# Three of four gate tensors of a conditioned block: from a product with ones to a DMA broadcast and a copy

## The chip, the cores and the metric

The kernel runs on one core of a Trainium2 chip. The metric is the device time of one execution in microseconds (us). All numbers are float32.

A core has engines that run side by side and wait for each other with semaphores: TensorE (PE in the profile, with PEld for its weight loads), VectorE (DVE), ScalarE (ACT) and GpSimd (POOL). DMAs are issued here from the queues of SyncE (SP) and of ScalarE (ACTq). SBUF is the on-chip memory; PSUM is where TensorE writes its products.

## The reference

`x` is (2, 2048, 512), the condition `t` is (2, 512). One linear layer makes six rows of 512 for each batch element; two of the six are gates:

```
emb = silu(t) @ ada_w + ada_b
shift_msa, scale_msa, gate_msa, shift_mlp, scale_mlp, gate_mlp = split(emb, 6)
norm  = ln(x) * (1 + scale_msa) + shift_msa
x     = x + gate_msa * (gelu(norm @ ssm_w1 + ssm_b1) @ ssm_w2 + ssm_b2)
norm2 = ln(x) * (1 + scale_mlp) + shift_mlp
x     = x + gate_mlp * (gelu_tanh(norm2 @ ff_w1 + ff_b1) @ ff_w2 + ff_b2)
```

The hidden width is 512 in the first part (called A) and 1024 in the second (called C).

## The kernel before

**Blocks and stages.** The rows of x are cut into eight blocks of 512; blocks 0 to 3 belong to batch element 0, blocks 4 to 7 to element 1. A block i goes through `Norm` 1 (statistics on DVE, scales on POOL, normalisation on ACT, turning of 32x32 pieces on DVE, moves by DMA between partitions, modulation with scale and shift on ACT at L508), then `First` (hidden values hA_i), `residual` (oA_i), `Norm` 2, `Second` (hidden values hC_i) and again `residual` (oC_i). The result in the profile is named after the stage: py_hA, px_oC and so on, where y, x and v are PSUM banks.

**Products.** Every matrix product is done as seven products of half-size quarters, P1 to P7, with sums of quarters ahead of it (nS, hSA, hSC; made by POOL or DVE at L311) and additions behind it. For hC of blocks 1 to 7 a longer list of such sums is used (L650, L712). A stage takes a dictionary of hooks: lists of operations that are written into the program right after the product P1, P2 and so on. The schedule is manual, so the order in the source is the order of every engine's queue, and `hook(hooks, ("P6",), ...)` is how the work around a product is placed. The stages for blocks 0 and 1 are written out one by one; from block 1's hC on there is one loop over blocks.

**Gates.** A gate never multiplies the output: it is folded into the second weight matrix of its part (w2 for gate 2, the fw2 matrix for gate 5), row by row, by DVE at L359 (`weight_of_second`), and into the second bias (`gb`, L830, L869, L632). For that it must stand in all 128 partitions, as a 128x512 tile `pgate` in PSUM. There are four such tiles: gates 2 and 5 for batch element 0, used near 21 and 57 us, and for element 1, used near 246 and 338 us, when w2 and fw2 are loaded again and folded again. `rows_of_gates` multiplies silu(t), padded to 32 columns, with the gate's 512 columns of ada_w, one product for each quarter of the depth, in four groups of 32 partitions; DVE adds the bias rows, and `make_gate` puts one batch row on all partitions by a product with a matrix that holds ones at that row of each group:

```
r = work.tile([P, D], F32, tag="grows", name=f"grows_{g}", bufs=2)
nc.vector.tensor_tensor(r, pa, brows[:, (2, 5).index(g), :], ALU.add)
...
nc.tensor.matmul(pg, pick_bc[:, b, :], gate_rows[g], start=True, stop=True)
```

The rows of shift and scale come from `modulation` (L261), sixteen products of 32x128 for each, turned by DVE (L271).

**Queues at the start.** ACT's queue holds four small loads of condition and biases (L225 to L228), the two loads of gate-bias rows (L240), then the load of the activation table, a dummy activation (L764), silu (L782) and the first normalisations. SP's queue holds the large loads: x in two halves (L202), six pieces of ada_w (L208), the weights (L215), rows of bias put on all partitions (`load_row`, L219) and later the moves (L485) and the stores. PE runs five products that nobody reads (L774) while it waits for data.

## Time and profile before

| | |
|---|---|
| median of 3 runs | 603.66 us (603.02 to 604.52) |
| the profiled execution | 603.54 us |
| its span, first to last instruction | 601.7 us |
| PE busy | 592.5 us, 2827 matmuls |
| DVE, ACT, POOL busy | 376.1, 218.7, 397.1 us |
| DMA | 49.31 MB; mean busy share of the 16 DMA engines 0.8 to 0.9 up to 45 us, later 0 to 0.6 |
| gate products `pgate` (L299) | 4, in 8 records of 0.59 us (the second record of a product starts before the first is drained) |
| copies of gate tensors on ACT | none |

A line of the profile names a line of the kernel, the engine, the operation, the tile that is written and those that are read (without buffer numbers), and the shape. In views in order of time the first two columns are the start and the length in us, and the brackets at the end hold the time for which the engine was idle before and what it waited for. In the view of waits the columns are the total, the number and the longest, in us. "x8" behind a matmul are records: a float32 product leaves two.

### The profile page before, as it was taken

Reading aid. Unit: us, or ns where it says so; the run is one execution under the profiler, and the core shown is the slowest. Engines: PE = TensorE matmul, PEld = TensorE weight load, DVE = VectorE, ACT = ScalarE, POOL = GpSimd, SP = SyncE. Lnnn points to the kernel's source line nnn. Section 1 sums busy time; section 2 is a strip of 40 time slices with the busy share of each in tenths; the row PEclk is TensorE's granted clock in tenths of the full one; section 3 lists DMA queues with packets and bytes.
Section 4 is the critical chain, followed back from the end, with each engine's and each line's share of the span. In section 5 each row is a group of like instructions: output and inputs, shape, how many; then the busy total and the mean of one; then the engine's idle time right before and its main releaser. Section 6 shows DMA issues by size and latency. Waiting matters only on the chain.

```text
span 601.7 us, 8144 instructions
## 1 busy us (share of the span) xinstructions
PE 592.5 (98%) x2827; PEld 509.8 (85%) x2827; DVE 376.1 (63%) x638; ACT 218.7 (36%) x363; POOL 397.1 (66%) x459
## 2 busy tenths in 40 slices
PE   8999999999999999999999999999999999999997
PEld 4787887887888888888888888888888888888886
DVE  5978988997754475645754458644565336467642
ACT  3234247304532254323731346123553225212420
POOL 2878688998735896549978398885983695540110
PEclk9999999999999999999999999999999999999999
DMA  8980222300223003340051611321020300022001
GB/s 323 413 349 14 58 71 70 106 35 36 52 89 105 36 2 87 141 139 1 5 140 52 202 42 28 113 70 71 1 58 14 105 36 0 2 54 88 1 0 70
DMA packets 23116, 49.31 MB, mean 82 GB/s; under 512 B 4340, under 2 KB 4896, under 8 KB 22180
## 3 DMA queue, kind: packets, MB, share of 16 engines
q1 hardware_dynamic: 20032, 44.58, 22.3%
q10 hardware_dynamic: 3044, 4.23, 2.7%
q8 instruction: 22, 0.36, 0.2%
q14 instruction: 18, 0.15, 0.1%
HBM read 25.72 MB, written 8.39 MB: 57 GB/s over the span
## 4 chain that ended last, share of the span: by engine, by line
PE 92%; DVE 2%; DMA 2%; POOL 1%; issue 1%; ACT 1%; ACTq 1%; SPq 0%; DVEq 0%
PE py_oC L391 18%; PE px_hC L712 10%; PE pv_oC L391 9%; PE py_hA L391 9%; PE py_oA L391 8%; PE pv_hC L712 8%; PE py_hC L712 8%; PE px_oC L391 5%; PE pv_hA L391 4%; PE pv_oA L391 4%; PE px_hA L391 2%; PE px_oA L391 2%; DMA ada<-in_L_cond_ada_w_dram 2%; PE py_hC L391 1%; PE pv_hC L391 1%
## 5 line engine op out<-in xcount | busy, mean ns | idle before, releaser
L625 POOL TENSOR_TENSOR x<-x,gb 128x512 f32<-128x512 f32 x64 | 79.8, 1279 | 9.4 <-DVE gb L869 3.5
L508 ACT ACTIVATE nT<-nT,mod,mod 128x512 f32<-128x512 f32 x54 | 39.6, 802 | 103.1 <-DMA nT<-blocks 103.1
L311 POOL TENSOR_TENSOR hSC<-hClo 128x512 f32<-128x512 f32 (+1 forms) x34 | 39.6, 1169 | 45.9 <-ACT hClo L707 37.8
L465 ACT ACTIVATE nT<-x,nmr,rstd 128x512 f32<-128x512 f32 x56 | 42.5, 803 | 58.7 <-POOL nmr L452 42.8
L434 POOL TENSOR_SCALAR ve<-mv 128x4 f32<-128x4 f32 x16 | 3.7, 231 | 86.6 <-DVE mv L426 86.4
L391 PE MATMUL py_oC<-fw_s,hSC 128*128 128x256 f32 x256 | 57.9, 379 | 0.0
L391 PEld LDWEIGHTS py_oC<-fw_s,hSC 128*128 128x128 f32 x256 | 48.6, 190 | 6.6
L613 DVE TENSOR_TENSOR x<-py_oC,x 128x512 f32<-128x512 f32 (+1 forms) x36 | 22.5, 628 | 40.7 <-PE py_oC L391 40.7
L425 DVE BATCH_NORM_STATS2 st<-x 128x6 f32<-128x512 f32 x64 | 43.4, 678 | 5.1 <-DMA x<-in_x_dram 4.8
L712 PE MATMUL py_hC<-forms,fw 128*128 128x256 f32 x168 | 40.8, 379 | 0.0
L476 DVE STREAM_TRANSPOSE blocks<-nT 128x512 f32<-128x512 f32 x56 | 37.7, 693 | 3.9 <-ACT nT L465 3.4
L729 DVE TENSOR_TENSOR hClo<-hClo,py_hC 128x512 f32<-128x512 f32 x42 | 28.5, 681 | 17.1 <-ACT hClo L726 9.4
L650 POOL TENSOR_TENSOR forms<-forms 128x256 f32<-128x256 f32 x48 | 35.4, 738 | 2.8
L712 PEld LDWEIGHTS py_hC<-forms,fw 128*128 128x128 f32 x168 | 31.9, 190 | 4.3
L613 DVE TENSOR_TENSOR x<-py_oA,x 128x512 f32<-128x512 f32 x32 | 22.0, 689 | 19.6 <-PE py_oA L391 19.0
L729 DVE TENSOR_TENSOR hChi<-hChi,pv_hC 128x512 f32<-128x512 f32 x35 | 23.3, 683 | 17.1 <-PE pv_hC L712 17.1
L391 PE MATMUL py_oA<-w_s,hSA 128*128 128x256 f32 x128 | 30.4, 381 | 0.2 <-DVE x L613 0.2
L391 PE MATMUL py_hA<-nS,w_s 128*128 128x256 f32 x128 | 30.4, 381 | 0.0
L707 ACT ACTIVATE hClo<-hClo,colsT 128x256 f32<-128x256 f32 x56 | 25.3, 500 | 11.5 <-DVE hClo L729 11.4
L391 PE MATMUL py_oC<-fw,hClo 128*128 128x256 f32 x128 | 28.9, 379 | 0.0
L391 PE MATMUL pv_oC<-fw,hClo 128*128 128x256 f32 x128 | 28.9, 379 | 0.0
L391 PE MATMUL py_oC<-fw_s,hChi 128*128 128x256 f32 x128 | 28.9, 379 | 0.0
(210 smaller groups left out, 1406.2 us busy)
## 6 DMA issues: line engine op xcount, KB each, us to landing
nT<-blocks SPq DMA_DIRECT2D x168, 64.0 KB, 2.0
out_dram<-x SPq DMA_DIRECT2D x15, 512.0 KB, 3.0
x<-in_x_dram SPq DMA_DIRECT2D x7, 1024.0 KB, 7.1
ada<-in_L_cond_ada_w_dram SPq DMA_DIRECT2D x6, 1024.0 KB, 9.5
fw<-in_L_cond_ff_w_dram SPq DMA_DIRECT2D x3, 2048.0 KB, 9.1
nT<-blocks ACTq DMA_DIRECT2D x56, 64.0 KB, 2.0
w<-in_L_cond_ssm_w_dram SPq DMA_DIRECT2D x3, 1024.0 KB, 7.4
x<-in_x_dram SPq DMA_DIRECT2D x2, 512.0 KB, 5.1
```

The lines of the kernel that those rows point to most:

```text
L311: eng.tensor_tensor(out[:, r], a[:, r], b[:, r], f)
L391: nc.tensor.matmul(ps[b][j * apart][:, j, :], lhs(p, j, k), rhs(p, j, k), start=(fresh and j * (not apart) == 0 and k == 0), stop=(p in (" ...
L425: nc.vector.bn_stats(st, xs[self.i][:, c, :])
L465: nc.scalar.activation(t, x_c, AF.Identity, bias=self.nmr[:, c : c + 1], scale=self.rstd[:, c : c + 1])
L476: nc.vector.transpose(self.bl[:, :, :, c, :].rearrange("p m k q -> p k m q"), self.nT[:, c, :].rearrange("p (k m q) -> p k m q", k=KD, m=C),)
L508: nc.scalar.activation(dst, src, AF.Identity, bias=shift, scale=scale)
L613: nc.vector.tensor_tensor(d, ps[BANK[p]][:, js], d, ALU.add)
L625: lambda c=c: nc.gpsimd.tensor_tensor(xs[i][:, c, :], xs[i][:, c, :], gb, ALU.add)
L650: eng.tensor_tensor(reg[d], reg[a], reg[b], ALU.add if f == "+" else ALU.subtract)
L707: nc.scalar.activation(h, h, AF.Gelu_apprx_tanh, bias=fb1T[:, m : m + 1])
L712: nc.tensor.matmul(ps[b][:, j, :], fa[ra][:, j * P : (j + 1) * P], fb[rb].rearrange("p a (c q) -> p c a q", q=Q), start=(fresh and j == 0) ...
L729: nc.vector.tensor_tensor(dest(d), dest(d), ps[b], op)
```

## The change

Gate 2 of batch element 0 is still put on all partitions by a product. The other three go another way: SP stores the gate rows to a scratch in DRAM (`store_gate`, four small stores), loads one row of 2 KB back to all 128 partitions (`load_gate`, tile gsb), and ACT copies it to PSUM (`sent_gate`). The gate rows themselves are made by the same sixteen 32x128 products as shift and scale (`rows_of`), so that their bias rows have another layout: eight small loads on ACT's queue in place of two. The one remaining product becomes four of 128x128. The first gate 5 (`ff_gate`) moves from the hook P3 of hA_1 to a place behind hA_1 and the moves of block 0, and with it the folding of its bias (`gb5_0`, from P1 to P5 of oA_1) and POOL's additions of this bias to block 0 (P1 and P7, now all at P7); two of POOL's four additions of gate 2's bias to block 2 move from P1 of hC_0 into hC_1.

```diff
-    nc.gpsimd.memset(brows[:, :2, :], 0.0)
+    nc.gpsimd.memset(brows[:, 0, : 2 * P], 0.0)
+    gate_b = {}
     for n, g in enumerate((2, 5)):
-        nc.scalar.dma_start(
-            out=brows[:B, n, :], in_=ada_b[g * D : (g + 1) * D].unsqueeze(0).to_broadcast([B, D])
-        )
+        gate_b[g] = brows[:, 0, n * P : (n + 1) * P]
+        for m in range(P // G):
+            row = ada_b[g * D : (g + 1) * D].rearrange("(n m q) -> m n q", n=KD, q=G)[m]
+            nc.scalar.dma_start(
+                out=gate_b[g][m * G : m * G + B, :].rearrange("p (n q) -> p n q", n=KD),
+                in_=row.unsqueeze(0).to_broadcast([B, KD, G]),
+            )
...
     def rows_of_gates(g):
...
+        pa = rows_of(g)
+        r = work.tile([P, P], F32, tag="grows", name=f"grows_{g}", bufs=2)
+        nc.vector.tensor_tensor(r, pa[:, :P], gate_b[g], ALU.add)
         gate_rows[g] = r
-    def make_gate(g, b):
+    def make_gate(g):
+        pg = ps_t.tile([P, D], F32, tag="t", name=f"pgate_{g}_0")
+        to = pg.rearrange("p (n m q) -> p m n q", n=KD, q=G)
+        for m in range(P // G):
+            nc.tensor.matmul(to[:, m], pick[:, m, :], gate_rows[g], start=(m == 0), stop=(m == P // G - 1))
+        gate[g, 0] = pg
+    def store_gate(g):
+        t = dram.tile([B, D], F32, tag=f"gdr_{g}", name=f"gdr_{g}")
+        to = t.rearrange("b (n m q) -> m b n q", n=KD, q=G)
+        for m in range(P // G):
+            rows_m = gate_rows[g][m * G : m * G + B, :].rearrange("p (n q) -> p n q", n=KD)
+            nc.sync.dma_start(out=to[m], in_=rows_m)
+        gate_dram[g] = t
+    def load_gate(g, b):
+        t = work.tile([P, D], F32, tag="gsb", name=f"gsb_{g}_{b}", bufs=1)
+        gate_sb[g, b] = load_row(t, gate_dram[g][b])
+    def sent_gate(g, b):
         pg = ps_t.tile([P, D], F32, tag="t", name=f"pgate_{g}_{b}")
-        nc.tensor.matmul(pg, pick_bc[:, b, :], gate_rows[g], start=True, stop=True)
+        nc.scalar.copy(pg, gate_sb[g, b])
         gate[g, b] = pg
...
-    hook(hooks, ("P6",), fold2(1, 7))
+    hook(hooks, ("P6",), fold2(1, 7) + [lambda: store_gate(2)])
...
-    hook(hooks, ("P6",), [lambda: rows_of_gates(5)])
+    hook(hooks, ("P6",), [lambda: rows_of_gates(5), lambda: store_gate(5)])
...
-    hook(hooks, ("P3",), [ff_gate])
...
+    load_gate(5, 0)
     n2[0].move((nc.scalar,), (2, 3))
+    ff_gate()
...
-    hook(hooks, ("P1",), hA_sums[2:3] + [gb5_0] + fw1_sums[3:] + gb5[:3])
+    hook(hooks, ("P1",), hA_sums[2:3] + fw1_sums[3:])
...
-    hook(hooks, ("P5",), n2_sums[:1] + [n1[2].scales])
-    hook(hooks, ("P7",), n2_sums[1:] + [lambda c=c: n1[2].normal(c) for c in range(C)] + gb5[3:])
+    hook(hooks, ("P5",), n2_sums[:1] + [n1[2].scales, gb5_0])
+    hook(hooks, ("P7",), n2_sums[1:] + [lambda c=c: n1[2].normal(c) for c in range(C)] + gb5)
...
-    hook(hooks, ("P1",), biases(2, gb[2]))
+    gb2_2 = biases(2, gb[2])
+    hook(hooks, ("P1",), gb2_2[:2])
...
+            hook(hooks, (5,), gb2_2[2:])
...
+        for g, ahead in ((2, 2), (5, 1)):
+            if (i + ahead) % PER_B == 0 and i + ahead < NBLK:
+                hook(hooks, (0,), [lambda g=g, b=(i + ahead) // PER_B: load_gate(g, b)])
...
-                hook(hooks, ("P1",), [lambda: make_gate(2, b)])
+                hook(hooks, ("P1",), [lambda: sent_gate(2, b)])
...
-            make_gate(5, b)
+            sent_gate(5, b)
```

The hook `(0,)` of the last addition stands in the products of hC_i, one or two blocks ahead of the use: the row of gate 2 for element 1 is loaded in block 2, that of gate 5 in block 3.

More of the change, by code (lines that the diff above doesn't have):

```diff
@@ L175 @@
     small = ctx.enter_context(tc.tile_pool(name="small", bufs=3))
+    dram = ctx.enter_context(tc.tile_pool(name="dram", bufs=1, space=bass.MemoryType.DRAM))
     ps_t = ctx.enter_context(tc.tile_pool(name="ps_t", bufs=2, space=bass.MemoryType.PSUM))
@@ L251, with rows_of @@
     mods = {}
-    def modulation(g0, part):
-        g = g0 + part
+    def rows_of(g):
         pa = ps_g.tile([P, D], F32, tag="x", name=f"pada_{g}")
@@ L269, in modulation @@
                 )
+        return pa
+    def modulation(g0, part):
+        g = g0 + part
+        pa = rows_of(g)
         turned = pa[:, P : 2 * P]
@@ L276, in modulation @@
         mods[g0, part] = m
-    gate, gate_rows = {}, {}
+    gate, gate_rows, gate_dram, gate_sb = {}, {}, {}, {}
     def rows_of_gates(g):
-        pa = ps_g.tile([P, D], F32, tag="x", name=f"pada_{g}")
-        for k in range(KD):
-            nc.tensor.matmul(
-                pa[k * G : (k + 1) * G, :],
-                silu[:, k, :],
-                ada[g][:, k, :],
-                start=True,
-                stop=True,
-                tile_position=(0, k * G),
-            )
-        r = work.tile([P, D], F32, tag="grows", name=f"grows_{g}", bufs=2)
-        nc.vector.tensor_tensor(r, pa, brows[:, (2, 5).index(g), :], ALU.add)
-        gate_rows[g] = r
-    def make_gate(g, b):
+        pa = rows_of(g)
+        r = work.tile([P, P], F32, tag="grows", name=f"grows_{g}", bufs=2)
+        nc.vector.tensor_tensor(r, pa[:, :P], gate_b[g], ALU.add)
+        gate_rows[g] = r
+    def make_gate(g):
[15 more added lines that the diff above has]
+    def sent_gate(g, b):
         pg = ps_t.tile([P, D], F32, tag="t", name=f"pgate_{g}_{b}")
-        nc.tensor.matmul(pg, pick_bc[:, b, :], gate_rows[g], start=True, stop=True)
+        nc.scalar.copy(pg, gate_sb[g, b])
         gate[g, b] = pg
@@ L790 @@
         nc.vector.tensor_scalar(rows_g, rows_g, 1.0, None, ALU.add)
-    pick = const.tile([P, B], F32, tag="pick", name="pick")
-    nc.vector.tensor_reduce(
-        pick,
-        ident.rearrange("p (k q) -> p q k", q=G)[:, :B, :],
-        axis=mybir.AxisListType.X,
-        op=ALU.add,
-    )
-    pick_bc = const.tile([P, B, P], F32, tag="pick_bc", name="pick_bc")
-    nc.vector.tensor_copy(pick_bc, pick.unsqueeze(2).to_broadcast([P, B, P]))
+    pick = const.tile([P, P // G, P], F32, tag="pick", name="pick")
+    nc.vector.tensor_copy(
+        pick, ident.rearrange("p (m q) -> p m q", q=G)[:, :, :1].to_broadcast([P, P // G, P])
+    )
     n1[0].scales(on_dve=True)
@@ L825, in ssm_gate @@
     def ssm_gate():
-        make_gate(2, 0)
+        make_gate(2)
         found["w2"] = weight_of_second(w2_sb, w2_s, gate[2, 0], (nc.vector,))
@@ L861, in ff_gate @@
     def ff_gate():
-        make_gate(5, 0)
+        sent_gate(5, 0)
         found["fw2"] = weight_of_second(fw2_sb, fw2_s, gate[5, 0], (nc.vector,), 4)
```

## The prediction

> **What bounds the kernel now.** I read the busy times of the page first, then the chain of work that ended last, then the waits of TensorE (PE).

> ```profile
> span 601.7 us, 8144 instructions
> PE 592.5 (98%) x2827; PEld 509.8 (85%) x2827; DVE 376.1 (63%) x638; ACT 218.7 (36%) x363; POOL 397.1 (66%) x459
> ...
> PE 92%; DVE 2%; DMA 2%; POOL 1%; issue 1%; ACT 1%; ACTq 1%; SPq 0%; DVEq 0%
> ...
> PE pada L261 <- DMA ada<-in_L_cond_ada_w_dram: 1.5, 1, 1.5
> ...
> PE py_hC L391 <- POOL nS L311: 0.5, 1, 0.5
> ```

> PE is the bound: a matmul removed from its queue is time won, if nothing else is late at that place. All of PE's waits together are under 6 us, and the two above are the ones that the change touches. So I followed two stretches in order of time. The first is the start:

> ```profile
> 2.46 2.58 ACTq L240 DMA_DIRECT2D brows<-in_L_cond_ada_b_dram  x2
> 4.80 0.69 DVE L425 BATCH_NORM_STATS2 st<-x 128x6 f32<-128x512 f32 x1 [4.80 <-DMA x<-in_x_dram]
> 5.07 1.28 ACT L764 ACT_TABLE_LOAD   x1 [5.07 <-DMA x<-in_x_dram]
> 8.42 0.22 ACT L782 ACTIVATE silu<-colsT 128x8 f32<-128x8 f32 x1 [1.85 <-POOL ve L434]
> 9.07 1.08 PE L261 MATMUL pada<-ada,silu 128*32 128x128 f32 x32
> ...
> 11.62 1.08 PE L261 MATMUL pada<-ada,silu 128*32 128x128 f32 x32 [1.46 <-DMA ada<-in_L_cond_ada_w_dram]
> ...
> 14.46 1.96 PE L391 MATMUL py_hA<-nT,w 128*128 128x256 f32 x8
> ```

> The two gate-bias loads of L240 stand on ScalarE's (ACT's) queue ahead of the table load and silu. The second was issued only at 4.80, when the first half of x landed (DVE starts on it at the same 4.80); the table load came right behind. The reason is in the built program: all DMAs share eight completion semaphores in turn, and a DMA that takes one up again waits on its own queue until the last DMA on it has landed. Here this wait is free, because silu waits for other data until 8.42 anyway. PE then waits for the second ada load until 11.62, starts on the first block at 14.46, and is fed almost without a gap from there.

> The second stretch is where the first gate of the feed-forward part is used:

> ```profile
> 56.87 1.02 PE L299 MATMUL pgate<-grows,pick_bc 128*128 128x512 f32 x2
> 57.73 1.89 PE L391 MATMUL py_hA<-nS,w 128*128 128x256 f32 x8
> ...
> 60.38 4.45 ACTq L485 DMA_DIRECT2D nT<-blocks  x7
> 66.52 2.93 ACT L508 ACTIVATE nT<-nT,mod,mod 128x512 f32<-128x512 f32 x4 [6.03 <-DMA nT<-blocks]
> 69.53 1.27 POOL L311 TENSOR_TENSOR nS<-nT 128x512 f32<-128x512 f32 x1 [1.85 <-ACT nT L508]
> 76.58 1.99 PE L391 MATMUL py_hC<-nS,fw_s 128*128 128x256 f32 x8 [0.46 <-POOL nS L311]
> ```

> This is a chain without slack: moves land, ACT modulates nT at 66.52, POOL forms sums from 69.53, and PE waits 0.46 us for them at 76.58.

> [...] the warm-up weight loads at the start stand 0.85 us apart (2.36, 3.21, 4.07), although that half of a 128x512 product takes 0.43 later, and at the end, where PE's last work is done 0.31 us into the stretch from 598, the granted clock has dropped in the last 0.7 us:

> ```profile
> 598.00:600.00 2.00, 0.31 (x2) 1.00 0.33 115
> 600.00:601.00 1.00, 0.00 (x0) 1.00 0.03 8
> 601.00:601.70 0.70, 0.00 (x0) 0.54 0.00 0
> ```

> (columns: stretch, its length, PE busy, clock granted, DMA share, GB/s).

> **The change part by part**, against the profiled execution's own 603.54 us (span 601.7), which lies 0.12 us from the median 603.66.

> 1. *Three gate products leave PE.* A product costs the distance to the next matmul: 57.73 - 56.87 = 0.86 us, and the same 0.86 at 245.63 and 338.04. The two late ones (gates of the second batch element) are gained in full, **-1.7 us**: their loads are issued 40 us and more ahead; the ACT copy falls behind the normalisation that ends at 251.6 and behind the modulation that ends at 336.9, both ACT stretches with idle time after them, and their first readers on DVE come at 255.42 and 344.89. The copy into PSUM isn't in the trace; an ACT instruction of this shape (L726) takes 0.60[...]. I take 0.6.

> 2. *Eight gate-bias loads in place of two on ACT's queue.* This part is the largest. In the built order, numbers 3 to 5 wait for small loads and the second half of x (all landed by 6.3), number 6 for the first ada load (issued at 1.62; the quickest ada load took 7.2, so about 8.9), **number 7 for the second ada load**, which lands at 11.6, number 8 for the first gate-bias load. An issue takes 0.3 to 0.4, so number 8 ends at about 12.3. Behind it on ACT: table load 1.28, a dummy activation 0.20, silu 0.22, so silu ends at about 14.1 instead of 8.64. PE gets both pada products from about 14.4 (silu to PE took 0.43), 1.0 each, and no longer waits for ada. DVE turns the first one 1.2 later (10.26 - 9.07) at 15.6, forms the modulation and then its two normalised rows to 17.0 (11.7 before), PE's sixteen transposes end at 18.6, and the modulated nT lets the block start at about 18.7. That is 4.2 us later than 14.46. What follows is fed by PE and shifts with it; the loads stay ahead, since their bytes keep the DMA busy in the same order.

> 3. *Half clock.* PE has nothing between 9.1 and 14.4, 5.3 us. At the end of the trace 2.7 us without work (598.31 to about 601) were enough, so a drop is likely here. Coming back took until between 7 and 8 us at the start, after work from 1.34. If PE runs 2 us of work at half clock, that costs 2 us; part of it hides behind the waits of point 2. Bounds 0 and 2.3; I take **1.0**, so **+5.2 us** for points 2 and 3.

> 4. *The first gate 5 by DMA.* Four stores on SP after the gate rows (DVE, about 53.8) are done before the moves start at 57.31; the output stores of 128 KB landed in 1.9. The load of the broadcast row comes behind SP's eight moves, at about 62.6. The trace has this very form: a bias row of 2 KB to 128 partitions, issued at 237.75 and 310.20 with little around it, landed 5.3 us after issue at the best. So it lands at about 68.0, and the copy, which stands ahead of the modulation on ACT, ends at 68.7 instead of the modulation starting at 66.52: +2.2. POOL and PE's wait at 76.58 follow. PE arrives 0.86 earlier there for the missing product and waits all the longer, so the first gate's gain is lost and **+2.2 us** stays. If the load needed only the 2.0 us of a move, the copy would fall into ACT's idle time before 66.52 (worth up to 0.3, because ACT's own moves start earlier); if it is slower than a bias row, 2.8.

> 5. *The rest, +0.1.* Gate rows as sixteen 32x128 products take about 1.0 us (L261: 11.62 to 12.62), as the four 32x512 did (18.08 to 19.07). The one remaining gate product becomes four of 128x128 with own weights, 8 records of about 0.11 (the transposes' pace), against 0.86. DVE's row addition shrinks, the pick copy doubles to some 0.5 beside a POOL wait that ends at 9.59, POOL's clearing is shorter. POOL's moved bias additions cost nothing: of gate 5, all four now come after the sums, and two of block 2 go later; that adds 1.2 us before 86.18, where POOL idled 2.14, and 2.5 before 155.36, where it idled 3.68. If those covers went, the statistics and the hidden sums behind them would be late by the excess.

> Sum: -1.7 + 5.2 + 2.2 + 0.1 = +5.8, so 603.6 + 5.8 = **609.4 us**.

> **Rivals.**
> - *The load is hidden* (25%): point 4 ends at -0.3, total 603.6 - 1.7 + 5.2 - 0.3 + 0.1 = 606.9. For it: ACT idles 6 us there. Against: both bias rows took 5.3.
> - *The start is covered* (8%): ACT isn't held by number 7, or something else sets 14.46. Then 603.6 - 1.7 + 2.2 + 0.1 = 604.2. Against: the 4.80 issue.
> - *Faster* (6%): the start is covered and the row lands by 65.9, in ACT's gap; -1.7 - 0.3 + 0.1 gives 601.7. It decides when the row lands within 3.3 us of issue and silu still ends by about 9.
> - *Worse* (6%): PE falls to half clock a second time in the wait before 76.58 (0.46 + 0.86 + 2.2 = 3.5 us long), another 2 to 3 us: 612.

> **How the numbers follow.** My case has 55%, with its own range 607.3 to 611.5 from the bounds of points 3 and 4. To hold 8 in 10, the range goes down past the hidden load and up to the worse case: 605.6 to 612.4. Less than 0.3% (1.8 us) either way can't be told from no change in three runs here: faster 0.06, same 0.08, slower 0.86.

> **What would show it.** Silu after 13.5, ACT's last gate-bias issue near 12.0, PE's first block near 18.7 and weight loads at double spacing before it prove points 2 and 3; silu near 8.4 refutes them. The copy near 68 plus the shift, and a PE wait of over 3 us on POOL at the first hC group, prove point 4. No L299-like gap before px_oC and py_hA of the later blocks proves point 1.

## The result, and the profile after

The changed kernel takes **608.25 us** (median of four runs: 608.06, 608.24, 608.26, 609.57) against 603.39 for the kernel before in the same comparison: a ratio of 1.0084, 95% interval 1.0066 to 1.0102. It is slower by 4.9 us where 5.8 was forecast. The profiled execution took 608.06 us, 4.5 more than the one before, and its span is 4.5 us longer.

The page and the waits of PE, after (a line of the waits has the total, the number and the longest, in us). Line numbers of the changed kernel are 4 to 22 higher:

```profile
span 606.2 us, 8266 instructions
PE 591.4 (98%) x2875; PEld 512.1 (84%) x2875; DVE 374.9 (62%) x637; ACT 220.0 (36%) x366; POOL 394.8 (65%) x459
...
PE pada L265 <- ACT silu L804: 4.8, 1, 4.8
PE py_hC L413 <- POOL nS L333: 2.0, 1, 2.0
```

PE works 1.1 us less than before and the span is longer all the same. Two waits have grown: pada waited 1.5 us for an ada load and now 4.8 for silu; py_hC waited 0.5 for POOL's sums and now 2.0. They are the two stretches that the prediction followed.

The start, after, in order of time:

```profile
2.53 9.87 ACTq L245 DMA_DIRECT2D brows<-in_L_cond_ada_b_dram  x8
12.43 1.28 ACT L786 ACT_TABLE_LOAD   x1 [12.43 <-DMA brows<-in_L_cond_ada_b_dram]
13.84 0.20 ACT L804 ACTIVATE silu<-colsT 128x8 f32<-128x8 f32 x1
14.09 3.61 PE L265 MATMUL pada<-ada,silu 128*32 128x128 f32 x64 [4.83 <-ACT silu L804]
16.48 2.43 DVE L491 TENSOR_SCALAR blocks<-x,rstd,nmr 128x512 f32<-128x512 f32 x2
18.97 1.64 PE L516 MATMUL pt<-ident,blocks 128*128 128x128 f32 x13 [0.80 <-DVE blocks L491]
20.45 0.81 PE L413 MATMUL py_hA<-nT,w 128*128 128x256 f32 x3
```

ACT's queue is busy with eight small loads until 12.40. Single instructions of the trace show why: numbers 5, 6 and 7 are issued at 6.54, 9.14 and 11.85, and the first and second ada load, whose semaphores numbers 6 and 7 take up again, have landed at 9.12 and 11.82. (The trace gives the semaphore of every DMA: all issues of SP and ACT carry one of eight numbers, 100 to 106 and 108, here 106 and 108. In the kernel before, the second gate-bias load, on 101, was issued at 4.80, and the first half of x, on 101 too, had landed at 4.78.) Silu ends at 14.04 instead of 8.64, and the first block starts at 20.45 instead of 14.46. The 64 records of both pada products take 3.61 us; 32 of them took 1.08 before. The granted clock, 0.50 in that stretch, explains it (columns: stretch, its length, PE busy and records, granted clock, DMA share, GB/s):

```profile
7.36:10.77 3.41, 1.90 (x5) 1.00 1.06 391
10.77:14.19 3.42, 0.10 (x4) 1.00 1.04 386
14.19:17.60 3.41, 3.41 (x64) 0.50 1.05 387
79.04:82.45 3.41, 1.83 (x9) 1.00 0.02 5
82.45:85.87 3.42, 3.02 (x14) 1.00 0.08 19
```

I cut the stretches at the borders that the clock record shows: half clock lasts from 14.19 to 17.60, 3.41 us, after 3.42 us with almost no work. The record changes at 7.36, 14.19, 17.60 and 608.11; these lie 6.83, 3.41 and 590.51 us apart, 2, 1 and 173 steps of 3.413 us, and the other borders are carried on at this step. The last two stretches hold the wait of 2.0 us ahead of py_hC; no half clock follows them.

The first gate 5, after:

```profile
65.43 4.46 ACTq L507 DMA_DIRECT2D nT<-blocks  x7
68.37 0.52 SPq L220 DMA_DIRECT2D gsb<-gdr  x1
72.10 0.59 ACT L321 COPY pgate<-gsb 128x512 f32<-128x512 f32 x1 [6.54 <-DMA nT<-blocks]
72.79 2.93 ACT L530 ACTIVATE nT<-nT,mod,mod 128x512 f32<-128x512 f32 x4
75.80 1.27 POOL L333 TENSOR_TENSOR nS<-nT 128x512 f32<-128x512 f32 x1 [9.88 <-ACT nT L530]
82.85 1.99 PE L413 MATMUL py_hC<-nS,fw_s 128*128 128x256 f32 x8 [1.98 <-POOL nS L333]
```

The row load is issued at 68.37 and the copy runs at 72.10, so the row landed in at most 3.7 us. (The view puts the copy's wait down to a move. The copy reads the row alone, whose semaphore is complete at 72.08; ACT's last move landed at 72.57, just before the copy ended at 72.69.) Modulation begins at 72.79, 6.27 later than before: the shift of the start (5.92 at this place) and only 0.35 on top.

One of the late gates. Before, a pgate product stood 0.86 us ahead of px_oC:

```profile
245.63 1.02 PE L299 MATMUL pgate<-grows,pick_bc 128*128 128x512 f32 x2
246.49 2.75 PE L391 MATMUL px_oC<-fw,hChi 128*128 128x256 f32 x12
```

After, px_oC follows py_oC directly:

```profile
248.76 3.19 PE L413 MATMUL py_oC<-fw,hClo 128*128 128x256 f32 x14
251.78 2.97 PE L413 MATMUL px_oC<-fw,hChi 128*128 128x256 f32 x13
```

Comparing the start of every PE stage with that of before gives the ledger. The delay is 5.99 us at the first block, 5.92 up to the place of the first gate 5, 6.26 after it (at py_hC), 5.30 from px_oC on (first late gate) and 4.43 from py_hA near 343 on (second). So: **start +5.9, first gate 5 +0.35, late gates -1.8**, together 4.4 of the 4.5 us.

### The profile page after: what moved, and what is told of

Same layout as the page of the kernel before. It is cut to its first block, busy times and chain, and to the rows that moved or that the text cites. A ratio compares the mean times of both kernels' runs of the same rounds, so it can differ in the third digit from the quotient of the medians.

```text
span 606.2 us, 8266 instructions
## 1 busy us (share of the span) xinstructions
PE 591.4 (98%) x2875; PEld 512.1 (84%) x2875; DVE 374.9 (62%) x637; ACT 220.0 (36%) x366; POOL 394.8 (65%) x459
## 4 chain that ended last, share of the span: by engine, by line
PE 91%; DVE 2%; DMA 2%; issue 1%; POOL 1%; ACT 1%; ACTq 1%; SPq 0%; DVEq 0%
PE py_oC L413 18%; PE px_hC L734 10%; PE pv_oC L413 9%; PE py_hA L413 9%; PE py_oA L413 8%; PE pv_hC L734 8%; PE py_hC L734 8%; PE px_oC L413 5%; PE pv_hA L413 4%; PE pv_oA L413 4%; PE px_hA L413 2%; PE px_oA L413 2%; DMA ada<-in_L_cond_ada_w_dram 2%; PE py_hC L413 1%; PE pv_hC L413 1%
## 5 line engine op out<-in xcount | busy, mean ns | idle before, releaser
L647 POOL TENSOR_TENSOR x<-x,gb 128x512 f32<-128x512 f32 x64 | 79.4, 1275 | 11.7 <-issue 8.7
L635 DVE TENSOR_TENSOR x<-py_oA,x 128x512 f32<-128x512 f32 x32 | 22.1, 690 | 19.3 <-PE py_oA L413 18.6
L413 PE MATMUL pv_oC<-fw,hSC 128*128 128x256 f32 x128 | 28.9, 379 | 0.0
L413 PE MATMUL px_oC<-fw,hChi 128*128 128x256 f32 x128 | 28.9, 379 | 0.0
```

The lines of the kernel that those rows point to most:

```text
L413: nc.tensor.matmul(ps[b][j * apart][:, j, :], lhs(p, j, k), rhs(p, j, k), start=(fresh and j * (not apart) == 0 and k == 0), stop=(p in (" ...
L635: nc.vector.tensor_tensor(d, ps[BANK[p]][:, js], d, ALU.add)
L647: lambda c=c: nc.gpsimd.tensor_tensor(xs[i][:, c, :], xs[i][:, c, :], gb, ALU.add)
```

## Experiments

My theory had three parts: the start is ACT's queue held by the waits of loads 6 to 8, plus half clock; the first gate 5 loses its product's gain in the chain moves, copy, modulation, sums; a late gate is worth one product. The rival to the first was that the new layout, the larger pick copy or SP's own loads make the start late. All ratios below are to the kernel before, measured on the same chip.

**E1: four gate-bias loads instead of eight.**

```diff
-        for m in range(P // G):
-            row = ada_b[...].rearrange("(n m q) -> m n q", n=KD, q=G)[m]
-            nc.scalar.dma_start(out=gate_b[g][m * G : m * G + B, :]..., in_=row...)
+        row = ada_b[...].rearrange("(n m q) -> m n q", n=KD, q=G)
+        for b in range(B):
+            nc.scalar.dma_start(out=gate_b[g][b::G, :].rearrange("m (n q) -> m n q", n=KD), in_=row)
```

> The changed kernel with its eight gate-bias loads written as four (one for each gate and batch row, over the four groups of partitions); the later loads of SP then take other semaphores. Theory (ACT's queue is held by loads 6 to 8, which wait for the first two ada loads): four loads wait for nothing later than x, silu ends near 8.6 instead of 14.04, PE starts on the first block near 14.5 instead of 20.45, and the whole shift of 5.9 us goes: 602.3 us, 1.1 below the kernel before. Rival (the start is late by the products' new layout, the pick copy on DVE or SP's own loads): silu may move, but the first block stays at 17 or later and the time above 605.

Measured: 603.69 us (12 runs), ratio 1.0004 (0.9995 to 1.0012). Silu ended at 8.49 and PE stood within 0.15 us of the kernel before from pada to the first gate 5: the whole shift of the start was gone. But the time was 1.4 above what I expected. Only two of the twelve runs took 602.32 and 602.37; their mean clock was 1.000. The other ten had 0.994 to 0.997. One stretch of 3.41 us at half clock lowers the mean over 602 us by 0.003, so by my estimate each of these ten had one or two; one of them has a profile. The stretches of E1 around the wait for POOL's sums (75.08 to 77.16):

```profile
74.92:78.33 3.41, 1.32 (x6) 1.00 0.02 5
78.33:81.75 3.42, 3.42 (x9) 0.50 0.26 60
```

The wait of 2.08 us lay in one stretch and left 1.32 us of work in it, and PE ran the next 3.42 us at a granted clock of 0.50, which costs 1.7 us, half of that stretch. In the changed kernel the wait was as long (1.98), but it was spread over two stretches with 1.83 and 3.02 us of work. That is the last rival of the prediction ("worse"), seen in E1 and not in the profiled run of the changed kernel.

**E2: six more small loads in the kernel before.** `for n in range(6): nc.scalar.dma_start(...)` behind its two gate-bias loads.

> The kernel before with six more small loads on ACT's queue behind its two gate-bias loads, into a part of the tile that nobody reads; nothing else of the change. Theory: the last loads wait for the first and second ada load, silu ends near 14, the first block starts near 20.4: 603.5 + 5.9 = 609.4 us. Rival (the rest of the change makes the start late): below 605.

Measured: 608.46 us, ratio 1.0082 (1.0067 to 1.0097). Silu ended at 13.76, the first block started at 20.21. The loads alone make the first block 5.75 us late, where the whole change made it 5.99. In this profiled run the half clock lasted twice as long (12.02 to 18.85), so the two starts are not alike in every part. It's E1 that shows that layout, pick and SP's loads make less than 0.15 us of the shift. The time was 0.9 below what I expected: 0.6 us of the shift is regained near 141 us, where the kernel before waits for ACT and this run does not.

**E3: six loads.** E1 with two more small loads that nobody reads.

> As the kernel with four gate-bias loads, with two more small loads behind them that nobody reads: the sixth waits for the first ada load (9.1 us), none for the second. Theory of the wait: the table load begins at 9.4, silu ends near 11.1, the first block starts near 15.9, 1.4 later than with four: 603.7 us. Rival (each load costs its own share, two of the four removed give half of the shift back): first block near 17.4, 605.3 us.

Measured: 604.88 us, ratio 1.0023 (1.0013 to 1.0033). The sixth load was issued at 9.06, silu ended at 10.94 and the first block started at 15.12, 0.66 later than before and less than either theory said. A further 0.8 us came later, of which 0.50 is a wait of the third pada product for its ada load (SP's loads now take other semaphores). The half clock in the wait for POOL's sums was there as in E1. The time alone lies nearer to the rival's 605.3; what decides against it is the first block, at 15.12 and not 17.4. So a load costs what it waits for (number 6 the first ada load, number 7 the second), not a share each.

**E4: PE kept busy until silu.** The changed kernel with `range(IDLE + 6)` in place of `range(IDLE)`.

> The changed kernel with six more of the warm-up products that nobody reads on PE ahead of the pada products, so that PE is busy until silu is there. Theory that the half clock adds to the start: the granted clock stays full from 14.2 to 17.6, pada and the transposes take their normal time, the first block starts near 18.8 and the time falls by 1.5 to 2 us, to 606.5. Rival (the stretch is set by DVE's turn, modulation and normalised rows, and the clock costs nothing there): within 0.4 us of 608.2.

Measured: 607.11 us, ratio 1.0063 (1.0048 to 1.0079). PE at the start of E4:

```profile
14.04 1.96 PE L265 MATMUL pada<-ada,silu 128*32 128x128 f32 x64 [0.40 <-ACT silu L804]
17.64 1.64 PE L516 MATMUL pt<-ident,blocks 128*128 128x128 f32 x13 [0.97 <-DVE blocks L491]
19.11 1.89 PE L413 MATMUL py_hA<-nT,w 128*128 128x256 f32 x8
```

The pada products took 1.96 us instead of 3.61, and the first block started at 19.11 instead of 20.45. Half clock was worth **1.34 us** of the start, less than the 1.5 to 2 that I expected (the medians lie 1.14 apart); the other 4.65 are the delay of silu and what DVE makes of it.

**E5: the copy behind the modulation.** E1 with `ff_gate` hooked behind `n2[0].moved()` in P6 of oA_1, and `gb5_0` in P7.

> The kernel with four gate-bias loads, with the copy of the first gate 5 placed behind the four modulations of block 0 on ACT's queue (before, it stood ahead of them) and the folding of its bias on DVE from P5 to P7 of oA_1. Theory (the copy's wait for the row load holds the modulation): modulation starts when ACT's moves have landed, near 65.8 instead of 67.11, POOL's sums follow, PE waits 0.8 us instead of 2.08 ahead of P6 of hC_0, no window of half clock follows: 602.3 - 1.3 = 601.0 us. Rival (the moves, not the copy, set the modulation): 67 stays, the wait stays near 2, and the time near 603.7. Rival (DVE stands at the folding until the late copy): a new PE wait for DVE in oA_1, over 602.

Measured: 604.54 us, ratio 1.0009 (0.9996 to 1.0022). My theory fell, and the first rival came true. Modulation began at 67.16, no earlier than E1's 67.11, although nothing stood ahead of it on ACT; PE waited 2.09 us, as in E1 (2.08). The chain of work that ended last names the last move ahead of it (start, length, what):

```profile
63.62 3.28 DMA nT<-blocks
```

In the kernel before, the same view has, ahead of the modulation at 66.52:

```profile
64.23 2.03 DMA nT<-blocks
```

The last move needs 3.28 us from its issue instead of 2.03. The row load, 256 KB issued by SP at 62.69, is under way at the same time. So it was not the copy that held the modulation, but late moves. That the bytes of the load make them late is what E10 tests.

**E10: the row load alone.** The kernel before with `load_row(forms[:, 8:10]..., fb2)` behind SP's moves.

> The kernel before with one more load of a bias row to 128 partitions (256 KB) behind SP's moves, into a place that nobody reads; no gate is changed, nobody waits for it. Theory (the load's bytes delay the last moves): modulation of block 0 starts 0.7 to 1.3 us later than 66.52, PE's wait at P6 of hC_0 grows from 0.46 to 1.2 to 1.7 us, the time by as much: 604.2 us. Rival (only the copy's wait costs, bytes nothing): 66.5, 0.46 and 603.2.

Measured: 604.30 us, ratio 1.0018 (1.0010 to 1.0026). The DMA issues of E10 from 57 to 70 us (the last number is the median from issue to landing, 2.0 for both queues in the kernel before):

```profile
nT<-blocks SPq DMA_DIRECT2D x8, 64.0 KB, 2.0
nT<-blocks ACTq DMA_DIRECT2D x8, 64.0 KB, 3.3
```

ACT's moves land 1.3 us later, SP's, which are ahead of the load, do not. The rival that the added load upsets the turn of the semaphores is ruled out by the issues: ACT's last seven moves were issued within 4.45 us, as before. In this profiled run the start was 1.55 us late through half clock; modulation began at 69.27, so 69.27 - 66.52 - 1.55 = **1.2 us** late for a load that nobody waits for. PE waited 1.6 us for POOL's sums instead of 0.46, as expected. From 63 to 68 us E10 moved 191 GB/s, and 262 KB at this rate are 1.4 us: by this estimate of mine the load's bytes can account for the delay. How the DMA engines divide their time between the two queues was not shown.

**E9: the row load ahead of ACT's moves.** E1 with the load issued by `nc.scalar` ahead of ACT's eight moves.

> The kernel with four gate-bias loads, with the row load of the first gate 5 issued from ACT's queue ahead of ACT's own eight moves instead of behind SP's moves: same bytes, same order of the copy ahead of the modulation. Theory (the 256 KB of this load run among the last moves and make them land 1.3 us late; where they run among the first, they cost ACT one issue of 0.5 us): the copy falls into ACT's idle time, modulation starts near 66.4 instead of 67.11, PE waits 1.3 to 1.4 us at P6 of hC_0 and no half clock follows in most runs: 601.7 us. Rival (the moves are late for another reason, or the load delays whatever is on its way): modulation at 67 or later, 603.7 us.

Measured: 604.11 us, ratio 1.0016 (1.0006 to 1.0027); modulation at 67.35. The chain of E9:

```profile
59.08 3.69 DMA gsb<-gdr
...
65.27 2.05 DMA nT<-blocks
```

The last move is quick again (2.05), as the theory had it. But ACT's fourth move was issued at 62.79 where the third had ended at 61.51. In the built program a move on ACT's queue takes up the completion semaphore of the row load, which landed at 59.08 + 3.69 = 62.77. What the bytes no longer cost, the wait on this semaphore does: the mechanism of the start, a second time. The rival came true: the moves were late for another reason.

**E7: the wait filled.** E1 with one product of 128x512 ahead of P6 of hC_0. It is written over what P1 left in the same bank, so the hidden values of block 0 come out different; the instructions that follow are the same.

> The kernel with four gate-bias loads, with one product of 128x512 that nobody reads on PE ahead of P6 of hC_0, inside its wait for POOL: work is added, nothing is taken away. Theory (the wait of 2.08 us leaves a window of 3.4 us with so little work that the next one runs at half clock, 1.7 us lost): 0.9 us of the wait is filled, no half clock follows in any run, 602.3 us. Rival (the runs at 603.7 are slower for another reason): 603.7, or more by the added product.

Measured: 602.24 us, ratio 0.9984 (0.9975 to 0.9992). 16 of 22 runs lie between 602.06 and 602.54. More work on PE made the kernel 1.4 us faster, since the stretch that held the wait now had 2.25 us of work and no half clock followed:

```profile
73.74:77.15 3.41, 2.25 (x9) 1.00 0.00 0
77.15:80.56 3.41, 3.37 (x16) 1.00 0.11 24
```

I had expected this of every run. The six other runs (603.36 to 604.16) have no profile; four of them had a mean clock of 0.997, by the estimate of E1 a stretch at half clock somewhere, and two had 1.000.

**E6: the first gate 5 by product again, the late two by DMA.** E1 with `ff_gate` in P3 of hA_1 and `make_gate(5)` in it, and the bias work of gate 5 and of block 2 at its former places.

> The kernel with four gate-bias loads, with the first gate 5 again made by a product in P3 of hA_1, and its followers on DVE and POOL at the places of the kernel before; only the two late gates go by DMA and a copy. Theory: PE's wait at hC_0 is 0.5 us as before, the two late products are gained in full: 603.2 - 1.7 + 0.1 = 601.6 us. Rival (the gain of the late gates is given back somewhere): near 603.2.

Measured: 602.38 us (22 runs), ratio 0.9984 (0.9975 to 0.9993). PE waited 0.64 us ahead of P6 of hC_0. In the trace PE is 0.43 us late there, 0.53 early from px_oC on and 1.39 early from the second late gate on: the gain of the late gates stays to the end. The time is 0.8 above what I expected. Eight of the runs lie between 603.70 and 604.25, six of them with a mean clock of 0.997.

**E8: all four gates by products in the new layout.** E6 with `make_gate(2, b)` and `make_gate(5, b)` in place of the copies, without the stores and the row loads; POOL makes a second matrix of ones.

> The kernel with four gate-bias loads, with all four gates made by products in the new layout (four of 128x128 each), no scratch in DRAM, no copies; a second matrix of ones is made by POOL while it has nothing else to do. Theory (a late gate by DMA is worth one product of 0.86 us): 1.7 us above the kernel that has only the first gate 5 by product, 603.3 us. Rival (the late products lie beside waits and cost nothing): 601.6.

Measured: 604.15 us, ratio 1.0012 (1.0000 to 1.0024), 1.77 above E6 where 1.7 was expected. Both kernels are 0.8 above their own forecasts, so that miss lies in what they share. Two products were worth 1.8 us, as the ledger has it. Against the kernel before, E8 is about half a microsecond late in the trace (0.27 at the first block, 0.48 at py_hC) and 0.9 by the medians (interval 0 to 1.4). How much of this the layout costs is open: E1 and E6 have the same start and are only 0.10 and 0.20 late at the first block.

**E11: POOL's order turned.** E9 with POOL's scales of block 2 behind the last sums for hC_0.

> As the kernel with the load ahead of ACT's moves, with POOL's eight small operations for block 2's scales (3 us) placed behind the last two sums of block 0 for hC_0 instead of between the first sum and them. Theory (the wait ahead of P6 is POOL's order: the sums would be ready at 74.8, before PE arrives at 75.1): the wait goes, the first product's 0.86 us is gained as well: 600.5 us. Rival (ACT's normalisation of block 2 is 4 us later, DVE stands at its turning and PE's results of hC_0 are fetched late): a wait for DVE of over 1 us at P5 or P7 of hC_0 in its place, 601.7 or more.

Measured: 607.34 us, ratio 1.0071 (1.0059 to 1.0083). The rival came true, and stronger. The wait ahead of P6 was gone (it started at 75.37), but the next py_hC, P7, shows, with DVE's line that precedes it:

```profile
80.51 1.42 DVE L498 STREAM_TRANSPOSE blocks<-nT 128x512 f32<-128x512 f32 x2 [5.97 <-ACT nT L487]
...
84.34 3.78 PE L413 MATMUL py_hC<-nS,fw_s 128*128 128x256 f32 x8 [5.35 <-DVE hClo L587]
```

DVE stands 5.97 us at the turning of block 2, ahead of PE's results in its queue; PE waits 5.35 us and then runs two stretches (81.89 to 88.71) at half clock.

**E12: the start filled.** E6 with one product that nobody reads between the first two pada products.

> The kernel with four gate-bias loads and the first gate 5 by product, with one product of 128x512 that nobody reads between the first two pada products, where PE waits 1.55 us for the second ada load. Theory (a stretch of 3.4 us with too little work at the start is what costs 1.5 us in 8 of 22 runs of the kernel without it): no run, or one in ten, above 603.4, median 602.2 us. Rival (those runs lose their time elsewhere): again about one run in three near 604, or the added product shifts the start by up to 0.9 us: 603.1.

Measured: 602.17 us, ratio **0.9980** (0.9971 to 0.9989), 11 of 12 runs between 602.01 and 602.56. It has the lowest ratio of all, 0.9 us below the kernel before (603.07 in this comparison), but E6 and E7 (0.9984) lie inside its interval. One run of 12 took over 603.3, where E6 had 8 of 22; so few runs make it likely, not certain, that the product removes them. E10's profile, whose start is that of the kernel before, shows what it would remove: PE had 1.25 us of work from 8.26 to 11.67, and the next 3.42 us ran at half clock. No such run of E6 has a profile, and two of its eight had a mean clock of 1.000, so half clock is not the reason of all of them.

## Why the prediction was right, and where it was off

The direction and the total were right: 608.25 us measured, 1.2 below the forecast of 609.4 and inside the range. The start is the largest part, as forecast. That the total came so close is in part luck: the start with its half clock was forecast 0.8 us too small, the first gate 5 1.85 too large.

- *Late gates, -1.7:* right. 0.96 and 0.87 in the trace, 1.77 between E8 and E6.
- *The start, +4.2:* right in its mechanism. Load 7 waited for the second ada load until 11.85 (forecast 11.6), silu ended at 14.04 (14.1), the last issue ended at 12.40 (12.3). E2 shows that the loads suffice, E1 that without them less than 0.15 us of the shift is left. A little was missing: E4, without half clock, starts the first block at 19.11 and not 18.7, because PE waits for DVE's normalised rows until 17.64 where I had 17.0. DVE's two rows took 1.95 us there and 0.99 before; why is open.
- *Half clock, +1.0:* 1.34 by E4, inside the bounds of 0 and 2.3.
- *The first gate 5, +2.2:* **this step failed**; it measured +0.35. Two terms were wrong. "The first gate's gain is lost" was not so: ACT's own moves stand behind the last activations of hA_1, which PE releases, so the missing product brought them forward too (64.78 against 59.72, a delay of 5.06 where PE had 5.92 just before). The prediction allowed 0.3 for this, and only if the load was quick. And the row load took 3.7 us, not the 5.3 of a bias row elsewhere in the trace. The cost then comes from a term that I did not have: the row load makes ACT's last moves late, and the modulation with them by 1.2 us (E10), and the copy ends just as they land. -0.86 + 1.2 = +0.35, within rounding. Neither of the two signs that were to prove the step was seen: the copy ran at 72.10 where 68 and the shift make 73.9, and the PE wait of "over 3 us" was 1.98.
- *The rest, +0.1:* not measured apart. E8, with all gates by product in the new layout, is 0.5 us late in the trace; in the changed kernel this part can't be told from the +5.9 of the start. The copy took 0.59 us (0.6 taken).
- *The range:* the bounds of points 3 and 4 give 611.3 at the top and, as long as the load is not hidden, 608.4 at the bottom. How 607.3 to 611.5 comes from them is not shown.

The 5.3 us came from a wrong reading of the trace. I took the two bias rows as landing "with little around" them, but each has a load of 1024 KB right behind it on the same queue, here the first (before):

```profile
237.75 0.53 SPq L219 DMA_DIRECT2D gb<-in_L_cond_ssm_b_dram  x1
238.39 0.40 SPq L202 DMA_DIRECT2D x<-in_x_dram  x1
```

The bias row of E10, beside moves of 64 KB, landed in 4.3 us. That the large load makes the difference was not tested.

Of the rivals, "the load is hidden" (606.9) was closer in size for this step (-0.3), but not its reason: hiding the copy gained nothing in E5 (modulation at 67.16, E1's at 67.11), where the load runs beside the moves. "Worse" was seen, after a shorter wait than forecast (2.08 us in E1, forecast 3.5): in the profiled runs of E1, E3, E5 and E9 half clock followed the wait, in that of the changed kernel, whose 1.98 us lay in two stretches, it did not. The changed kernel's run of 609.57 had a mean clock of 0.990 against 0.997 in the others; it has no profile, so that it is the same cause is not shown.

## What to carry to other kernels

Count the DMAs on a queue, not only their bytes. Where completion semaphores are used in turn, look up which earlier DMA had the semaphore that a small load takes up: here two small loads were issued at 9.14 and 11.85, right after two of 1024 KB had landed (9.12 and 11.82), and silu, behind them on ACT's queue, ended 5.4 us later. A transfer that "has time" can still delay those that have none: in E10 a load of 256 KB that nobody waits for brought ACT's moves in 1.3 us later. Look for what else is in flight when it lands. And where PE must wait, look at how much work is left in the stretch of the clock record that holds the wait: with 1.32 of 3.41 us (E1) the next stretch ran at half clock, 1.7 us on top of the wait, and with 2.25 (E7) it did not. There a product that nobody reads was worth its place: 602.24 against 603.69 us.

## What the hardware showed that I had not expected

- A wait of 2.08 us was followed by half clock (E1). The stretches of half clock here are 3.41 us or twice that, unless the run ends first (0.19 us at the end of after). Cut in steps of 3.413 us from the changes of the clock record, the stretch before a drop held 0.10 us of work (start, after), 1.32 (E1) and 1.25 (E10); stretches at full clock with 1.57 (E7, from 8.88), 1.83 and 1.90 (both after) were followed by full clock. A stretch that itself ran at half clock, with 1.61 us of work (E2, from 12.02), was followed by half clock again. What decides was not shown: no stretch with work between 1.32 and 1.57 us was measured.
- The same kernel has runs with and without the drop: E1 took 602.3 to 602.4 in two runs, at a mean clock of 1.000, and 603.6 to 605.0 in ten, at 0.994 to 0.997.
- A row of 2 KB put on 128 partitions took 3.7 us from issue to landing beside the moves (3.69 in E9; 4.3 for the bias row of E10), and added 1.3 us to the moves of the other queue (E10).
